# A gated graph network and a graph attention layer: two transposes moved from TensorE to DMA, a broadcast moved from DMA to TensorE

## The chip, the cores and the metric

The kernel runs on one core of one Trainium2 chip. A core has five engines that are of interest here: TensorE (PE in the profile: matrix products, and transposes as products with an identity), VectorE (DVE), ScalarE (ACT), GpSimd (POOL) and SyncE (SP), which issues nearly all of the DMAs. Each engine runs its own instructions strictly in their order and waits on semaphores for those of others. The metric is the device time in microseconds, lower is better.

## The reference

There are 64 graphs of 256 nodes with 256 features, in float32. Layer 0 is a gated graph network of three steps, layer 1 one step of graph attention; each starts from a layer norm and a relu, and is added to its input.

```python
h = relu(layernorm(x)); h0 = h                  # "first h" of a graph
for i in range(3):
    m = h @ weight[i]
    aggr = A.T @ m                              # A = (adj != 0)
    h = gru_cell(aggr, h, w_ih, w_hh, b_ih, b_hh)
x = x + h
h = relu(layernorm(x)) @ W.T
e = leaky_relu((h @ a_left)[:, :, None] + (h @ a_right)[:, None, :])
e = where(adj == 0, -1e9, e)
x = x + softmax(e, axis=-1) @ h
```

## The kernel before, in words

Graphs go through two at a time (G = 2), in 32 pairs. A tile of class "full" or "round" is 128 partitions by 512 elements: either the two halves of one graph's nodes with nodes on partitions, or both graphs of the pair with half of the features on partitions ("transposed").

Layer 0 works on the transposed form. First h comes out of the norm with nodes on partitions (`norm_relu`, L498) and is transposed ("turn 0", "turn 1", L525: four 128x128 transposes on TensorE for each half of the features, then a copy out of the bank by ScalarE, "turn copy", L529). In each of three steps `split` (L316, L443 to L445) cuts h into parts in a rounded format, "prop" (L543) multiplies by the adjacency, and `gate` (L458, the scale on ScalarE L472, L463) forms the gates; "back" (L586) transposes h back to nodes on partitions.

Layer 1: after the second norm VectorE forms the left and right scores of each node ("dot", L608) as columns of a small tile. The right scores have to stand along the free axis of all partitions. Before, for all pairs but the last, they are written as a line to DRAM ("line", L617) and read back as a broadcast over 128 partitions ("right", L620); in the last pair TensorE transposes the column spread over 128 columns (L628). "leaky" on ScalarE (L632) adds left and right and applies the leaky relu, "mask" (L635) and "max" (L637) run on VectorE, "exps" (L644) on ScalarE for both graphs. The attention weights are transposed ("p turn", L659: four TensorE transposes a graph; "p copy", L663: ScalarE), multiplied by h ("mix", L668), projected by W ("project", L677), added ("out", L682) and stored (L685).

The order of the instructions is not written by hand. Every operation is entered in a `Plan` with its engine, the time it occupies the engine, a latency, its reads and writes and the fixed leads of a table. `Plan.run` then places the operations one by one, always the one that can start earliest, over a window of four pairs, so that layer 1 of one pair is interleaved with layer 0 of the next ones; tiles are handed out in the same pass, from 28 tiles "full", 32 "round" and 8 PSUM banks. The start of an operation follows from these lines:

```python
for q in o.preds:
    t = max(t, q.start + q.occ if q.eng == e else q.end)
```

The costs in the plan decide the order alone; on the chip each engine runs in this order and waits for what is late.

Of the kernel before, what the change touches and what calls it, by code (L numbers as in the profile page):

```python
# [10 lines left out]
F32 = mybir.dt.float32  # L11
F32R = mybir.dt.float32r
I32 = mybir.dt.int32
AF = mybir.ActivationFunctionType
ALU = mybir.AluOpType
AX = mybir.AxisListType
# [176 lines left out]
def tile_gated_gnn_then_gat(  # L193
# [35 lines left out]
    nc = tc.nc  # L229
    P = 128  # L230
# [4 lines left out]
    G = 2  # L235
# [12 lines left out]
    plan.slot_class("x", [const.tile([P, GN], F32, name=f"x{i}") for i in range(2)])  # L248
    plan.slot_class("adj", [const.tile([P, GN], I32, name=f"adj{i}") for i in range(2)])
    plan.slot_class("small", [const.tile([P, 32], F32, name=f"small{i}") for i in range(12)])  # L250
    dram = ctx.enter_context(tc.tile_pool(name="dram", bufs=1, space=bass.MemoryType.DRAM))
    plan.slot_class("line", [dram.tile([1, N], F32, name=f"line{i}") for i in range(4)])
    plan.slot_class("bank", [psum.tile([P, GN], F32, name=f"bank{i}") for i in range(8)])

    ALL = (0, 1)
# [193 lines left out]
    def gate(name, e, terms, tops, apart=False, bias=0.0):  # L449
# [24 lines left out]
        pe(name + " rest", 2 * PASS * len(terms), rest, r=reads((2,), 1), w=[(bank, ONE)])  # L474
        return bank

    def norm_relu(name, src, dst):

        sm = Buf("small")
        st = lambda k: sm.t[:, 6 * k : 6 * k + 6]  # L480
        mv = lambda: sm.t[:, 12:16].rearrange("p (k s) -> p k s", s=2)

        def stats():
            for nb in range(NB):
                nc.vector.bn_stats(st(nb), parts(src)[:, nb, :])
            for nb in range(NB):
                nc.vector.bn_aggr(mv()[:, nb, :], st(nb))

        dve(name + " stats", 900, stats, r=[(src, ALL)], w=[(sm, (0, 1))])
        dve(name + " eps", 70, lambda: nc.vector.tensor_scalar(sm.t[:, 16:18], mv()[:, :, 1], LN_EPS, None, op0=ALU.add),  # L490
            r=[(sm, (0, 1))], w=[(sm, (2,))])
        pool(name + " pow", 900, lambda: nc.gpsimd.tensor_tensor(sm.t[:, 16:18], sm.t[:, 16:18], nhalf, ALU.pow),  # L492
             r=[("nhalf", ONE)], w=[(sm, (2,))])
        dve2(name + " shift", 70, lambda: nc.vector.scalar_tensor_tensor(sm.t[:, 18:20], mv()[:, :, 0], -1.0, sm.t[:, 16:18],
                                                       op0=ALU.mult, op1=ALU.mult),
            r=[(sm, (0, 1, 2))], w=[(sm, (3,))])
        for nb in range(NB):
            act(name + " relu", 495, lambda nb=nb: nc.scalar.activation(  # L498
                parts(dst)[:, nb, :], parts(src)[:, nb, :], AF.Relu,
                bias=sm.t[:, 18 + nb : 19 + nb], scale=sm.t[:, 16 + nb : 17 + nb]),  # L500
                r=[(src, (nb,)), (sm, (2, 3))], w=[(dst, (nb,))])

    def pair(p):
# [12 lines left out]
            dve2(f"in lo {g}", V512, lambda g=g, hi=hi, lo=lo: nc.vector.tensor_sub(lo[g].t, h[g].t, hi[g].t.bitcast(F32)),  # L516
                r=[(h[g], ALL), (hi[g], ONE)], w=[(lo[g], ONE)])
        hT = [Buf("full") for _ in range(DB)]
        for db in range(DB):
            pt = Buf("bank")  # L520

            def turn(db=db, pt=pt):
                for g in range(G):
                    for nb in range(NB):
                        nc.tensor.transpose(pt.t[:, (g * NB + nb) * P : (g * NB + nb + 1) * P],  # L525
                                            parts(h[g])[:, nb, ts(db, P)], ident)

            pe(f"turn {db}", TR * 4, turn, r=[(b, ALL) for b in h] + [("ident", ONE)], w=[(pt, ONE)])
            act(f"turn copy {db}", A512, lambda db=db, pt=pt: nc.scalar.copy(hT[db].t, pt.t), r=[(pt, ONE)], w=[(hT[db], ALL)])  # L529
# [71 lines left out]
        for g in range(G):  # L601
            pool("fill", 520, lambda b=pm_[g]: nc.gpsimd.memset(b.t, NEG_INF), w=[(pm_[g], ALL)])
            norm_relu(f"mid {g}", XR[g], hb[g])
            sm = sms[g]
            for nb in range(NB):
                for n in range(2):
                    c = 12 + n * NB + nb
                    dve2(f"dot {g}", 425, lambda g=g, nb=nb, n=n, c=c, sm=sm: nc.vector.scalar_tensor_tensor(  # L608
                        parts(sc[g])[:, nb, :], parts(hb[g])[:, nb, :], 1.0, va[:, n, :], op0=ALU.mult, op1=ALU.mult,
                        accum_out=sm.t[:, c : c + 1]),  # L610
                        r=[(hb[g], (nb,)), ("va", ONE)], w=[(sm, (c,)), (sc[g], (nb,))])

            if p < NPAIR - 1:
                line, pR = Buf("line"), Buf("full")
                plan.op(f"line {g}", "SP", 150, 2800, lambda line=line, sm=sm: nc.sync.dma_start(  # L617
                    line.t.rearrange("o (nb q) -> (o q) nb", q=P), sm.t[:, 12 + NB : 12 + 2 * NB]),
                    r=[(sm, (14, 15))], w=[(line, ONE)])
                plan.op(f"right {g}", "SP", 150, 2600, lambda line=line, pR=pR: nc.sync.dma_start(  # L620
                    pR.t[:, :N], line.t.to_broadcast([P, N])), r=[(line, ONE)], w=[(pR, ONE)])
            else:
                pR = Buf("bank")

                def right(sm=sm, pR=pR):
                    for nb in range(NB):
                        c = 12 + NB + nb
                        nc.tensor.transpose(pR.t[:, ts(nb, P)], sm.t[:, c : c + 1].to_broadcast([P, P]), ident)  # L628

                pe(f"right {g}", 2 * TR, right, r=[(sm, (14, 15))], w=[(pR, ONE)])  # L630
            for nb in range(NB):
                act(f"leaky {g}", 365, lambda b=sc[g], nb=nb, pR=pR, sm=sm: nc.scalar.activation(  # L632
                    parts(b)[:, nb, :], pR.t[:, :N], AF.Prelu, bias=sm.t[:, 12 + nb : 13 + nb], alpha=LEAKY_SLOPE),
                    r=[(pR, ONE), (sm, (12 + nb,))], w=[(sc[g], (nb,))])
            dve2(f"mask {g}", 660, lambda g=g: nc.vector.copy_predicated(pm_[g].t, A[g].t.bitcast(I32), sc[g].t),  # L635
                r=[(A[g], ONE), (sc[g], ALL)], w=[(pm_[g], ALL)])
            dve(f"max {g}", 610, lambda b=pm_[g], sm=sm: nc.vector.tensor_reduce(sm.t[:, 0:NB], parts(b), AX.X, ALU.max, negate=True),  # L637
                r=[(pm_[g], ALL)], w=[(sm, ONE)])
# [11 lines left out]
        for g in range(G):  # L650
            sm = sms[g]
            dve("recip", 70, lambda sm=sm: nc.vector.reciprocal(sm.t[:, 8 : 8 + NB], sm.t[:, 4 : 4 + NB]),
                r=[(sm, (1,))], w=[(sm, (2,))])
            pt, pT, pg, ag, pv = Buf("bank"), Buf("full"), Buf("bank"), Buf("full"), Buf("bank")

            def turn(g=g, pt=pt):
                for jb in range(NB):
                    for ib in range(NB):
                        nc.tensor.transpose(pt.t[:, (jb * NB + ib) * P : (jb * NB + ib + 1) * P],  # L659
                                            parts(pm_[g])[:, ib, ts(jb, P)], ident)  # L660

            pe(f"p turn {g}", 4 * TR, turn, r=[(pm_[g], ALL)], w=[(pt, ONE)])
            act(f"p copy {g}", A512, lambda pt=pt, pT=pT: nc.scalar.copy(pT.t, pt.t), r=[(pt, ONE)], w=[(pT, ONE)])  # L663

            def mix(g=g, pT=pT, pg=pg):
                for db in range(DB):
                    for jb in range(NB):
                        nc.tensor.matmul(pg.t[:, ts(db, N)], parts(hb[g])[:, jb, ts(db, P)], pT.t[:, ts(jb, N)],  # L668
                                         start=(jb == 0), stop=(jb == NB - 1))

            pe(f"mix {g}", 4 * MM, mix, r=[(pT, ONE), (hb[g], ALL)], w=[(pg, ONE)])
            act(f"mix copy {g}", A512, lambda ag=ag, pg=pg: nc.scalar.copy(ag.t, pg.t), r=[(pg, ONE)], w=[(ag, ONE)])

            def project(ag=ag, pv=pv):
                for ib in range(NB):
                    for db in range(DB):
                        nc.tensor.matmul(pv.t[:, ts(ib, D)], ag.t[:, db * N + ib * P : db * N + (ib + 1) * P],  # L677
                                         wT[:, db, :], start=(db == 0), stop=(db == DB - 1))

            pe(f"project {g}", 4 * MM, project, r=[(ag, ONE)] + WT, w=[(pv, ONE)])  # L680
            for nb in range(NB):
                dve(f"out {g}", VP256, lambda b=XR[g], nb=nb, pv=pv, sm=sm: nc.vector.scalar_tensor_tensor(  # L682
                    parts(b)[:, nb, :], pv.t[:, ts(nb, D)], sm.t[:, 8 + nb : 9 + nb], parts(b)[:, nb, :],
                    op0=ALU.mult, op1=ALU.add), r=[(pv, ONE), (sm, (2,))], w=[(XR[g], (nb,))])
            dma("store", 256, lambda g=g, b=XR[g]: nc.sync.dma_start(rows(out, G * p + g), parts(b)), r=[(XR[g], ALL)])  # L685
# [36 lines left out]
```

## Time and profile before

| | |
|---|---|
| runs | 2807.66 us median of 3 (2804.49 to 2813.82) |
| profiled execution | 2807.66 us, its span 2805.9 us |
| TensorE busy | 2312.1 us, 82% |
| VectorE busy | 1832.8 us, 65% |
| ScalarE busy | 1677.4 us, 60% |
| TensorE clock granted, mean | 0.898 |
| right broadcast, x62 | 128 KB, 4.8 us from issue to landing |
| line, x62 | 1 KB, 9.1 us from issue to landing |
| turn, TensorE, x256 | 39.9 us busy; its copy on ScalarE x64, 585 ns each |
| p turn, TensorE, x256 | 35.8 us busy; its copy on ScalarE x64, 591 ns each |

In a line of waits the engine and its tile and line stand first, then what it waited for, then the sum of the waits in us, how many they are, and the longest. In a line of a timeline the first two numbers are the start and the duration in us, and what stands in brackets is the idle time before it. A matmul's duration contains the pipeline, so the distance between starts is the better measure of its cost.

### The profile page before, as it was taken

How to read it: one execution, taken by the hardware profiler on the slowest of the kernel's cores; microseconds unless marked ns; L12 is line 12 of the kernel's file. 1: busy time of each engine (PE TensorE's matmuls, PEld its weight loads, DVE VectorE, ACT ScalarE, POOL GpSimd, SP SyncE). 2: the span in 40 equal slices, each digit the busy share in tenths (PEclk: the TensorE clock that was granted, in tenths of full speed). 3: DMA queues.
4: the chain of work that ended last, by engine and by line, in shares of the span. 5: the costliest groups of instructions: out<-in, count | busy, mean ns of one | idle time of the engine just before them, and what ended most of it. 6: DMA issues, size and time to landing. Idle time of an engine off the chain costs nothing. (4 is left out here: it accounts for less than half of the span.)

```text
span 2805.9 us, 30945 instructions
## 1 busy us (share of the span) xinstructions
PE 2312.1 (82%) x10853; PEld 1886.9 (67%) x10853; DVE 1832.8 (65%) x4084; ACT 1677.4 (60%) x3069; POOL 136.8 (5%) x198
## 2 busy tenths in 40 slices
PE   8987778877789777897777987778977789877786
PEld 6766667766677666676666776667766667666665
DVE  8766666765667556676566766566765667666654
ACT  8665556655656556566565665565655656655654
POOL 1000000000000000000000000000000000000000
PEclk9988889988899888999888988889988999889897
DMA  2011111111111111111111111111111111111001
GB/s 83 23 34 19 23 31 32 32 27 21 25 33 32 31 23 19 34 31 34 19 20 34 32 33 24 22 28 33 32 31 23 19 35 31 34 19 23 16 18 25
DMA packets 98332, 79.93 MB, mean 28 GB/s; under 512 B 22128, under 2 KB 98176, under 8 KB 98176
## 3 DMA queue, kind: packets, MB, share of 16 engines
q1 hardware_dynamic: 98144, 77.95, 12.3%
q8 instruction: 85, 1.39, 0.2%
q14 instruction: 71, 0.58, 0.1%
q10 hardware_dynamic: 32, 0.01, 0.0%
HBM read 61.09 MB, written 16.84 MB: 28 GB/s over the span
## 5 line engine op out<-in xcount | busy, mean ns | idle before, releaser
L458 PE MATMUL bank<-round,fac_hh 128*128 128x512 f32 x2304 | 698.7, 434 | 298.5 <-ACT round L443 297.9
L458 PEld LDWEIGHTS bank<-round,fac_hh 128*128 128x128 f32 x2304 | 461.8, 209 | 405.4 <-ACT round L443 311.2
L458 PE MATMUL bank<-round,fac 128*128 128x512 f32 x2304 | 617.6, 402 | 0.0
L463 PE MATMUL bank<-round,fac_hh 128*128 128x512 f32 x1152 | 397.4, 427 | 156.6 <-ACT bank L472 156.6
L458 PEld LDWEIGHTS bank<-round,fac 128*128 128x128 f32 x2304 | 443.0, 193 | 104.6
L472 ACT ACTIVATE bank<-bank 128x512 f32<-128x512 f32 x576 | 332.7, 583 | 126.5 <-PE bank L458 123.8
L635 DVE COPY_PREDICATED full<-round,full 128x512 f32<-128x512 int32 x64 | 46.7, 730 | 512.5 <-ACT full L632 512.4
L632 ACT ACTIVATE full<-full,small 128x256 f32<-128x256 f32 x124 | 59.4, 503 | 527.5 <-DMA full<-line 527.5
L463 PE MATMUL bank<-round,fac 128*128 128x512 f32 x1152 | 372.6, 410 | 2.5 <-ACT bank L472 2.5
L463 PEld LDWEIGHTS bank<-round,fac_hh 128*128 128x128 f32 x1152 | 206.0, 195 | 213.7 <-ACT bank L472 184.8
L443 ACT CAST round<-full 128x512 fp32r<-128x512 f32 x384 | 234.5, 620 | 109.9 <-DVE full L316 109.9
L444 DVE TENSOR_TENSOR round<-full,full 128x512 fp32r<-128x512 f32 x384 | 261.9, 689 | 9.6
L463 PEld LDWEIGHTS bank<-round,fac 128*128 128x128 f32 x1152 | 221.3, 195 | 60.2 <-ACT bank L472 11.5
L445 DVE SCALAR_TENSOR_TENSOR round<-round,full 128x512 fp32r<-128x512 f32 x384 | 255.0, 685 | 3.4
L575 DVE TENSOR_TENSOR full<-full,full 128x512 f32<-128x512 f32 x192 | 132.3, 689 | 136.4 <-ACT full L569 136.3
L543 PE MATMUL bank<-round,round 128*128 128x256 f32 x1536 | 216.2, 283 | 0.7 <-DVE round L594 0.7
L543 PEld LDWEIGHTS bank<-round,round 128*128 128x128 f32 x1536 | 206.1, 189 | 15.0 <-DVE round L594 0.9
L566 ACT ACTIVATE full<-full,vec 128x512 f32<-128x512 f32 x192 | 138.9, 723 | 98.0 <-DVE full L565 94.2
L565 DVE TENSOR_TENSOR full<-full,bank 128x512 f32<-128x512 f32 x192 | 131.6, 686 | 74.4 <-PE bank L463 67.2
L492 POOL TENSOR_TENSOR small<-small,nhalf 128x2 f32<-128x2 f32 x128 | 97.0, 758 | 1626.5 <-DVE small L490 1530.4
L316 DVE TENSOR_SCALAR full<-full 128x512 int32<-128x512 int32 (+1 forms) x400 | 163.0, 421 | 10.8 <-ACT full L547 5.0
L594 DVE TENSOR_TENSOR round<-bank,round 128x512 fp32r<-128x512 f32 x128 | 87.9, 688 | 117.7 <-ACT round L593 115.5
(75 smaller groups left out, 2883.2 us busy)
## 6 DMA issues: line engine op xcount, KB each, us to landing
x<-in_x_dram SPq DMA_DIRECT2D x64, 256.0 KB, 2.8
adj<-in_adj_dram SPq DMA_DIRECT2D x64, 256.0 KB, 2.7
full<-in_x_dram SPq DMA_DIRECT2D x64, 256.0 KB, 3.1
out_dram<-full SPq DMA_DIRECT2D x64, 256.0 KB, 2.1
full<-line SPq DMA_DIRECT2D x62, 128.0 KB, 4.8
line<-small SPq DMA_DIRECT2D x62, 1.0 KB, 9.1
full<-in_L_gnn_w_ih_dram SPq DMA_DIRECT2D x3, 256.0 KB, 4.0
full<-in_L_gnn_weight_dram SPq DMA_DIRECT2D x3, 256.0 KB, 4.7
```

What stands on the lines that cost most here:

```text
L316: dve2(name, 60 + n * 0.54, lambda: nc.vector.tensor_scalar(dst().bitcast(I32), src().bitcast(I32), CUT, None, op0=ALU.bitwise_and), r=r, w=w)
L443: act(name + " 0", C512, lambda: nc.scalar.copy(v0.t, t.t), r=[(t, ONE)], w=[(v0, ONE)])
L444: dve2(name + " 1", V512, lambda: nc.vector.tensor_sub(v1.t, v.t, t.t), r=[(v, ALL), (t, ONE)], w=[(v1, ONE)])
L445: dve2(name + " d", V512, lambda: nc.vector.scalar_tensor_tensor(vd.t, v1.t.bitcast(F32), -SPLIT, t.t, op0=ALU.mult, op1=ALU.add), r=[(v1, ...
L458: nc.tensor.matmul(bank.t, f(m, j, kb), b.t, start=(first and n == 0), stop=True, skip_group_check=True)
L463: nc.tensor.matmul(bank.t, f(m, 2, kb), s[kb][2].t, start=False, stop=True, skip_group_check=True)
L472: act(name + " scale", A512, lambda: nc.scalar.activation(bank.t, bank.t, AF.Identity, bias=bias, scale=1.0 + C), r=[("vec", ONE)], w=[(ba ...
L492: pool(name + " pow", 900, lambda: nc.gpsimd.tensor_tensor(sm.t[:, 16:18], sm.t[:, 16:18], nhalf, ALU.pow), r=[("nhalf", ONE)], w=[(sm, (2 ...
L543: nc.tensor.matmul(pa.t[:, ts(g, N)], parts(b)[:, sb, ts(db, P)], parts(A[g])[:, sb, :], start=(n == 0), stop=(n == len(terms) - 1))
L565: dve(f"u add {db}", V512, lambda u=u, k=pn: nc.vector.tensor_add(u.t, u.t, k.t), r=[(pn, ONE)], w=[(u, ONE)])
L566: act(f"tanh {db}", 615, lambda u=u, en=en: nc.scalar.activation(u.t, u.t, AF.Tanh, bias=b_i[:, en : en + 1]), r=[("vec", ONE)], w=[(u, ONE)])
L575: dve2(f"d mul {db}", V512, lambda d=d, b=z_: nc.vector.tensor_mul(d.t, d.t, b.t), r=[(z_, ONE)], w=[(d, ALL)])
```

## The change

Two things are done together. Right scores are spread by TensorE in all pairs, as they were in the last one, and the DRAM line and its tiles are gone. First h (for all pairs but the first) and the attention weights (for all pairs but the last) are no longer transposed by TensorE. Instead the 32-bit tile is seen as 16-bit halves: one DMA transpose turns 128 x 1024 halves into eight blocks of 128 x 128, in which low and high halves stand on alternating partitions; eight plain DMAs gather the even and odd partitions of each block to where they belong, low and high halves in separate columns; and a copy on ScalarE, over 1024 16-bit elements, interleaves them again ("join"). All of these DMAs are issued by SyncE.

```diff
-    plan.slot_class("line", [dram.tile([1, N], F32, name=f"line{i}") for i in range(4)])
+    def dma_turn(name, src, dst, region):
+        t = Buf("full")
+        view = lambda: t.t.bitcast(U16).rearrange("p (k c n) -> p k c n", k=NB, n=P)
+        plan.op(name, "SP", 200, 4500, lambda: nc.sync.dma_start_transpose(
+            t.t.bitcast(U16).rearrange("p (c n) -> p c n", n=P), src.t.bitcast(U16)), r=[(src, ALL)], w=[(t, ONE)])
+        def gather(c):
+            for q in range(2):
+                for half in range(2):
+                    nc.sync.dma_start(dst(c, slice(64 * q, 64 * q + 64))[:, half].rearrange("p (k n) -> p k n", k=NB),
+                                      view()[half::2, :, 2 * c + q, :])
+        for c in range(2):
+            plan.op(name + " gather", "SP", 500, 3500, lambda c=c: gather(c), r=[(t, ONE)], w=[region(c)])
+    def join(name, src, dst):
+        act(name, 980, lambda: nc.scalar.copy(
+            dst.t.bitcast(U16).rearrange("p (j n b) -> p j n b", j=2, b=2),
+            src.t.bitcast(U16).rearrange("p (j b n) -> p j n b", j=2, b=2)), r=[(src, ALL)], w=[(dst, ALL)])
...
-        for db in range(DB):
+        if p > 0:
+            rs = [Buf("full") for _ in range(DB)]
+            for g in range(G):
+                dma_turn(f"turn {g}", h[g], lambda db, rows, g=g, rs=rs: rs[db].t[rows].bitcast(U16).rearrange(
+                    "p (g b n) -> p g b n", g=G, b=2)[:, g], lambda db, g=g, rs=rs: (rs[db], (g,)))
+            for db in range(DB):
+                join(f"turn copy {db}", rs[db], hT[db])
+        for db in range(DB if p == 0 else 0):
...
-            if p < NPAIR - 1:
-                line, pR = Buf("line"), Buf("full")
-                plan.op(f"line {g}", "SP", 150, 2800, lambda line=line, sm=sm: nc.sync.dma_start(
-                    line.t.rearrange("o (nb q) -> (o q) nb", q=P), sm.t[:, 12 + NB : 12 + 2 * NB]),
-                    r=[(sm, (14, 15))], w=[(line, ONE)])
-                plan.op(f"right {g}", "SP", 150, 2600, lambda line=line, pR=pR: nc.sync.dma_start(
-                    pR.t[:, :N], line.t.to_broadcast([P, N])), r=[(line, ONE)], w=[(pR, ONE)])
-            else:
-                pR = Buf("bank")
-                def right(sm=sm, pR=pR):
-                    for nb in range(NB):
-                        c = 12 + NB + nb
-                        nc.tensor.transpose(pR.t[:, ts(nb, P)], sm.t[:, c : c + 1].to_broadcast([P, P]), ident)
-                pe(f"right {g}", 2 * TR, right, r=[(sm, (14, 15))], w=[(pR, ONE)])
+            pR = Buf("bank")
+            def right(sm=sm, pR=pR):
+                for nb in range(NB):
+                    c = 12 + NB + nb
+                    nc.tensor.transpose(pR.t[:, ts(nb, P)], sm.t[:, c : c + 1].to_broadcast([P, P]), ident)
+            pe(f"right {g}", 2 * TR, right, r=[(sm, (14, 15))], w=[(pR, ONE)])
...
-            pe(f"p turn {g}", 4 * TR, turn, r=[(pm_[g], ALL)], w=[(pt, ONE)])
-            act(f"p copy {g}", A512, lambda pt=pt, pT=pT: nc.scalar.copy(pT.t, pt.t), r=[(pt, ONE)], w=[(pT, ONE)])
+            if p < NPAIR - 1:
+                rs = Buf("full")
+                dma_turn(f"p turn {g}", pm_[g], lambda jb, rows, rs=rs: rs.t[rows].bitcast(U16).rearrange(
+                    "p (j b n) -> p j b n", j=NB, b=2)[:, jb], lambda jb, rs=rs: (rs, (jb,)))
+                join(f"p copy {g}", rs, pT)
+            else:
+                pe(f"p turn {g}", 4 * TR, turn, r=[(pm_[g], ALL)], w=[(pt, ONE)])
+                act(f"p copy {g}", A512, lambda pt=pt, pT=pT: nc.scalar.copy(pT.t, pt.t), r=[(pt, ONE)], w=[(pT, ALL)])
```

In the order that the planner makes of the changed kernel, SyncE's queue for one pair reads: two transposes of attention weights, their 16 gathers, two stores, two loads of x, a load of adj, the transpose of first h of one graph, its 8 gathers, a load of x and of adj, the transpose of first h of the other graph, its 8 gathers, a load of x.

More of the change, by code (lines that the diff above doesn't have):

```diff
@@ L13 @@
 I32 = mybir.dt.int32
+U16 = mybir.dt.uint16
 AF = mybir.ActivationFunctionType
@@ L250, in tile_gated_gnn_then_gat @@
     plan.slot_class("small", [const.tile([P, 32], F32, name=f"small{i}") for i in range(12)])
-    dram = ctx.enter_context(tc.tile_pool(name="dram", bufs=1, space=bass.MemoryType.DRAM))
-    plan.slot_class("line", [dram.tile([1, N], F32, name=f"line{i}") for i in range(4)])
     plan.slot_class("bank", [psum.tile([P, GN], F32, name=f"bank{i}") for i in range(8)])
@@ L653, in pair @@
                 r=[(sm, (1,))], w=[(sm, (2,))])
-            pt, pT, pg, ag, pv = Buf("bank"), Buf("full"), Buf("bank"), Buf("full"), Buf("bank")
+            pT, pg, ag, pv = Buf("full"), Buf("bank"), Buf("full"), Buf("bank")
+            pt = Buf("bank")
             def turn(g=g, pt=pt):
@@ L669, in mix @@
                                          start=(jb == 0), stop=(jb == NB - 1))
-            pe(f"mix {g}", 4 * MM, mix, r=[(pT, ONE), (hb[g], ALL)], w=[(pg, ONE)])
+            pe(f"mix {g}", 4 * MM, mix, r=[(pT, ALL), (hb[g], ALL)], w=[(pg, ONE)])
             act(f"mix copy {g}", A512, lambda ag=ag, pg=pg: nc.scalar.copy(ag.t, pg.t), r=[(pg, ONE)], w=[(ag, ONE)])
```

## The prediction

> **What bounds the kernel now.** I read the waits first, because TensorE is busy for 82% of the span and the question is what the rest is.
>
> ```profile
> ACT full L632 <- DMA full<-line: 527.5, 62, 15.6
> DVE full L635 <- ACT full L632: 512.4, 61, 15.3
> PE bank L458 <- ACT round L443: 297.9, 30, 15.2
> PE bank L463 <- ACT bank L472: 159.1, 38, 13.0
> ```
>
> 62 times (twice in each of 31 pairs) ScalarE stands for 8.5 us until the broadcast of the right-hand scores lands. TensorE's two large idle groups (297.9 and 159.1 us, together 14.7 a pair) name ScalarE's cast and scale, which are queued behind that wait. Then stretches of 10 us, columns PE, PEld, DVE, ACT, POOL busy, granted clock, DMA share, GB/s:
>
> ```profile
> 1000.00:1010.00 10.00, 2.66 (x15) 1.94 (x13) 0.50 (x1) 1.38 (x3) 0.00 (x0) 0.74 0.07 14
> 1010.00:1020.00 10.00, 3.78 (x8) 2.48 (x8) 2.78 (x5) 2.42 (x6) 0.00 (x0) 0.50 0.28 13
> 1020.00:1030.00 10.00, 8.27 (x33) 6.77 (x34) 9.04 (x17) 9.94 (x21) 1.26 (x2) 0.74 0.00 0
> 1030.00:1040.00 10.00, 10.00 (x49) 8.50 (x48) 6.07 (x11) 5.97 (x12) 0.00 (x0) 1.00 0.03 9
> 1040.00:1050.00 10.00, 10.00 (x51) 8.36 (x50) 4.43 (x9) 4.91 (x9) 0.00 (x0) 1.00 0.32 97
> ```
>
> Outside the two waits TensorE is never idle and has its full clock; inside them it is idle, and the clock falls to 0.50 and stays there for some 4 us after work resumes. Summed by microsecond over 87 us, a pair's period (86.25 us: the 31 first broadcasts are issued from 139.24 to 2726.84) is 67.2 us of TensorE work at full clock, 15.3 idle and 3.75 lost to the half clock. The timelines of ScalarE around the place where the change puts new waits:
>
> ```profile
> 1062.42 1.08 ACT L498 ACTIVATE full<-x,small 128x256 f32<-128x256 f32 x2
> ...
> 1067.01 0.59 ACT L498 ACTIVATE full<-x,small 128x256 f32<-128x256 f32 x1
> ...
> 1070.12 0.63 ACT L443 CAST round<-full 128x512 fp32r<-128x512 f32 x1
> 1070.64 0.67 ACT L472 ACTIVATE bank<-bank,vec 128x512 f32<-128x512 f32 x1
> ```
>
> First h of the two graphs is ready at 1063.5 and 1067.6, seven microseconds before the instruction at 1070.64.
>
> **What the Trainium skill says.** "TensorE: Matmul & The Clock Gate", What's actually happening: after an idle window of about 3.4 us the clock halves. The trace agrees: 0.50 from 2 to 4 us into each gap. "DMA: Bandwidth & Descriptors", Issuing engines are not separate DMA queues, and Two DMAs through the same engine are not ordered: a dependent DMA has to wait, on the issuing engine, for the first one's completion. The trace shows this: SyncE waits 554.9 us in 62 times for the first DMA of the pair (line) before it issues the second.
>
> **Why the planner did not see the stall, before or after.** `Plan.run` lets an operation start after a predecessor on its own engine at `q.start + q.occ`, after others at `q.end`. Line and right are both SP operations, so right is planned 150 ns after line, and line's 2800 are never counted. The changed kernel has the same pattern: a transpose and its gathers are all SP, so the gathers are planned 200 ns after the transpose; its 4500 counts nowhere. ScalarE's joins stand too early by a whole DMA transpose.
>
> **The change, part by part, for one pair.** T is the time from issue to landing of one DMA transpose of 256 KB, which no trace here shows.
>
> 1. Removed: the line and right DMAs, with 15.3 us idle and 3.75 of half clock.
> 2. TensorE: 16 transposes fewer (turn and p turn; four start within 0.36 us, 1068.34 to 1068.70, so 1.44 us), 4 more for right (0.36). Work 67.2 - 1.1 = 66.1 us. The new right can wait for VectorE's dots in TensorE's queue; VectorE is 65% busy, I cost that at nothing, up to 1 us a pair without that cover.
> 3. ScalarE: four joins of 1024 elements for four copies of 585 and 591 ns. From 384 elements at 530 ns (L377) and 512 at 620 (L443), 0.70 ns an element, a join takes 980 ns; the page "ScalarE: Activation LUTs", What ACT_TABLE_LOAD costs, gives 186 + 0.833 x 1024 = 1039. I take 1.0. The 1.6 us more hide in ScalarE's 40% idle time except where it is late, which is counted below.
> 4. SyncE: 4 transposes and 32 gathers for 4 DMAs. A load occupies the queue for 0.37 us (row of L305); 8 gathers take 3.0. A load of 256 KB lands in 2.8 us, with 16 packets on each DMA engine at 54 ns (share 0.32 of 160 engine-us for 97 GB/s of 1 KB packets), so 1.9 is fixed. A gather has 8 packets an engine: 1.9 + 0.4 = 2.3 us.
> 5. Attention weights. From the end of exps (time 0) ScalarE has five scales, a cast, a table load (1.28) and a sigmoid ahead of the first join, at the starts seen (0.5 each, 0.6 the sigmoid) 4.9 us. Graph 0's weights are ready at -1.1; transposed at T - 1.1; 8 gathers issued by T + 1.9, landed T + 4.2. Wait: T - 0.7. Graph 1's gathers go behind them on the queue: landed T + 7.1, 1.9 after the first join's end. TensorE stands at mix 0 for the whole first wait; mix 0 itself (1.7 us) covers part of the second: 1.2 idle. Sum T + 0.5.
> 6. First h. The first transpose is issued at 1063.5; its gathers block SyncE until T has passed, then take 3.0, then two loads 0.74; only now, at 1067.2 + T, does the second transpose go. It lands at 1067.2 + 2T; four gathers 1.5 and 2.3: 1071.0 + 2T. The join's place on ScalarE, behind the same L443, is 1070.6. Wait: 2T + 0.4. TensorE has 4.0 us of released work by then, and ScalarE needs 3.0 after the wait (join, copy, join, scale) to release more: 2T - 0.6 idle.
>
> Idle in all 3T - 0.1 us a pair. For T the lower bound is a load of the same bytes, 2.8; the page "Advanced Engine Details and Errata", X-Bar Transpose (TRN2), calls transposes as fast as regular DMAs. The upper one is eight blocks in a row at the 1309 ns of "VectorE: DVE Perf Modes", The three transpose paths: 10.5. I take 4.3, an estimate: 1.9 fixed, 1.0 for the bytes at the 261 GB/s of "DMA: Bandwidth & Descriptors", Latency and other measured facts, and 1.4 for descriptors of 256 bytes. Idle is then 12.8, the half clock costs 3.4 (the first gap is shorter than before's), the period is 66.1 + 12.8 + 3.4 = 82.3 us: 3.95 less than 86.25, x31 = 122. The span of 2805.9 becomes 2684. The profiled run took 2807.66, which is also the median of the three runs, 1.8 more than its span: 2686 us.
>
> **Rivals.** *Slow transposes*: new idle passes the old at T = 5.5 (16.4 + 3.8 against 15.3 + 3.75 + 1.1), and each further us costs 3 x 31 = 93 us. For it: nothing hides T, and it is serial twice at first h. Against it: the pages' bandwidths. T = 7.5 gives 22.4 + 4: 3004 us; 10.5 gives 3290. *Transposes like loads*: T = 2.8, idle 8.3, half clock 2.5: 2519 us. *Hidden anyway*: the gathers' latency is planned and h is wanted by the splits only some 3 us later, so if ScalarE reached the joins late enough, little would be left; S = 2 gives 2246. Against it, the tight places of steps 5 and 6. *Slow gathers*: packets of 256 bytes landing like line's (9.1 us, median) would add 6.8 twice, 13.6 us a pair, 3108 us; but line writes 4-byte pieces to HBM, the gathers 256 bytes to SBUF.
>
> **How the numbers follow.** Within 0.3%, about 8 us, is about what a measurement of this kernel can tell from no change. My case (T from 3.3 to 5.3; its own range 2565 to 2790) has 0.42, T lower or partly hidden 0.15, slow transposes 0.29, slow gathers or a new queue wait 0.10, and 0.04 falls within 0.3% around T = 5.5. Faster 0.57, same 0.04, slower 0.39. The range from 2450 to 3060 leaves out the fully hidden case and T over 8.
>
> **What would show it.** Right: no wait for a broadcast; two waits of ScalarE a pair ending on gathers, one of about T + 2 after exps, one of about 2T at first h, with the second transpose issued only after the first's gathers; TensorE's clock at 0.50 in two places a pair; transposes landing in 4 to 5 us. Wrong: T outside 3 to 5.5; gathers landing over 3 us; SyncE busy for more than 0.4 us a gather; joins much over 1 us; or ScalarE reaching the joins so late that it waits for nothing.

## The result

| | before | changed |
|---|---|---|
| median | 2806.07 us (2803.83 to 2813.82) | 2850.98 us (2843.94 to 2853.46) |
| ratio | | 1.0151, 95% interval 1.0123 to 1.0179 |
| span of the profiled execution | 2805.9 us | 2847.4 us |
| TensorE busy | 2312.1 us | 2325.8 us |
| mean clock granted | 0.898 | 0.902 |

The kernel became 1.5% slower; the interval is clear of 1. 2686 us and "faster" were forecast. The time lies inside the range of 2450 to 3060 us, but above the time of the kernel before, not below it. In the waits of the changed kernel the broadcast is gone, and the joins stand where it stood:

```profile
ACT full L496 <- DMA full<-full: 569.6, 123, 11.9
PE bank L462 <- ACT bank L471: 301.1, 32, 11.3
PE bank L697 <- ACT full L496: 177.1, 62, 5.4
```

ScalarE waits 18.4 us a pair at the joins (569.6 over 31; before 17.0 at the broadcast). TensorE's idle time is again in two groups: 301.1 us behind the joins of first h (its gates wait for the scale, L471, which stands behind the joins), and 177.1 us at mix (L697), which reads the joined weights. Together 15.4 us a pair, against 14.7 in the two groups of before. The stretches of 10 us, in the columns of before:

```profile
1000.00:1010.00 10.00, 6.56 (x40) 5.46 (x38) 5.95 (x13) 1.59 (x3) 0.69 (x1) 1.00 0.42 102
1010.00:1020.00 10.00, 3.66 (x9) 2.88 (x10) 4.19 (x12) 5.07 (x8) 0.79 (x1) 0.58 0.20 51
1020.00:1030.00 10.00, 10.00 (x46) 8.22 (x45) 8.40 (x24) 8.96 (x18) 0.00 (x0) 0.91 0.00 1
1030.00:1040.00 10.00, 10.00 (x48) 8.12 (x47) 9.93 (x23) 8.65 (x19) 0.00 (x0) 1.00 0.17 33
1040.00:1050.00 10.00, 6.25 (x26) 4.75 (x25) 3.81 (x6) 5.29 (x7) 0.00 (x0) 0.95 0.30 63
1050.00:1060.00 10.00, 7.91 (x20) 5.77 (x19) 2.67 (x4) 5.12 (x8) 0.99 (x2) 0.53 0.05 11
```

Two gaps a pair, each followed by a stretch at half clock. Summed by microsecond over three whole periods, a pair is 66.7 us of TensorE's work at full clock, 16.0 idle and 5.0 lost to the half clock; the same sum over three periods of the kernel before gives 67.5, 15.3 and 4.05. The gain in TensorE's work (0.8 us) is there; idle time and half clock took back more than that.

What fills the gaps is seen on SyncE's queue (start, duration of the whole row; L482 is the transpose, L488 the gather, L304 a load) and beside it on ScalarE (L521 makes first h, L665 is exps, L496 the join):

```profile
994.54 1.27 SPq L482 DMA_TRANSPOSE full<-full  x1
997.67 5.17 SPq L488 DMA_DIRECT2D full<-full  x8
1002.88 0.60 SPq L304 DMA_DIRECT2D x<-in_x_dram  x1
1003.58 0.41 SPq L304 DMA_DIRECT2D adj<-in_adj_dram  x1
1004.08 1.27 SPq L482 DMA_TRANSPOSE full<-full  x1
1008.10 5.17 SPq L488 DMA_DIRECT2D full<-full  x8
...
1037.11 2.64 SPq L482 DMA_TRANSPOSE full<-full  x2
1040.40 10.35 SPq L488 DMA_DIRECT2D full<-full  x16
```

```profile
993.44 1.08 ACT L521 ACTIVATE full<-x,small 128x256 f32<-128x256 f32 x2
...
1012.09 1.16 ACT L496 COPY full<-full 128x1024 uint16<-128x1024 uint16 x1 [10.38 <-DMA full<-full]
...
1037.48 0.50 ACT L665 ACTIVATE full<-full,small 128x256 f32<-128x256 f32 x1
...
1047.15 1.16 ACT L496 COPY full<-full 128x1024 uint16<-128x1024 uint16 x1 [2.53 <-DMA full<-full]
1052.36 1.16 ACT L496 COPY full<-full 128x1024 uint16<-128x1024 uint16 x1 [4.05 <-DMA full<-full]
```

First h of the first graph is ready at 994.52. The second graph's transpose goes at 1004.08 only, after the first one's landing, its eight gathers and two loads; the join starts at 1012.09, after a wait of 10.38. The weights (transposes at 1037.11, then all 16 gathers) cost two waits, 2.53 and 4.05. Eight gathers occupy the queue for 5.17 us: this is the number that was not foreseen.

### The profile page after: what moved, and what is told of

Its sections match the earlier page's. It is cut to its first block, busy times and chain, and to the rows that moved or that the text cites. A ratio compares the mean times of both kernels' runs of the same rounds, so it can differ in the third digit from the quotient of the medians.

```text
span 2847.4 us, 32298 instructions
## 1 busy us (share of the span) xinstructions
PE 2325.8 (82%) x10481; PEld 1878.3 (66%) x10481; DVE 1829.1 (64%) x4084; ACT 1731.4 (61%) x3069; POOL 130.1 (5%) x198
## 4 chain that ended last, share of the span: by engine, by line
PE 40%; SPq 16%; DMA 13%; DVE 13%; ACT 12%; issue 5%; ACTq 0%; DVEq 0%; POOLq 0%; POOL 0%
PE bank L457 19%; SPq L488 16%; DMA full<-full 13%; PE bank L462 9%; PE bank L706 4%; PE bank L573 3%; PE bank L697 3%; DVE round L444 2%; ACT bank L471 2%; DVE round L443 2%; ACT full L521 2%; DVE small L508 1%; ACT full L496 1%; ACT L665 1%; ACT full L665 1%
## 5 line engine op out<-in xcount | busy, mean ns | idle before, releaser
L457 PE MATMUL bank<-round,fac_hh 128*128 128x512 f32 x2304 | 643.3, 408 | 2.0 <-DVE round L443 2.0
L462 PE MATMUL bank<-round,fac_hh 128*128 128x512 f32 x1152 | 388.4, 419 | 300.8 <-ACT bank L471 300.8
L457 PEld LDWEIGHTS bank<-round,fac 128*128 128x128 f32 x2304 | 472.6, 206 | 116.0 <-ACT round L442 0.7
L496 ACT COPY full<-full 128x1024 uint16<-128x1024 uint16 x124 | 144.0, 1161 | 569.6 <-DMA full<-full 569.6
L457 PEld LDWEIGHTS bank<-round,fac_hh 128*128 128x128 f32 x2304 | 427.4, 192 | 89.2 <-DVE round L443 2.5
L462 PEld LDWEIGHTS bank<-round,fac_hh 128*128 128x128 f32 x1152 | 210.3, 195 | 345.7 <-ACT bank L471 309.0
L471 ACT ACTIVATE bank<-bank 128x512 f32<-128x512 f32 x576 | 328.6, 583 | 162.1 <-PE bank L457 156.1
L462 PE MATMUL bank<-round,fac 128*128 128x512 f32 x1152 | 348.1, 396 | 0.3 <-ACT bank L471 0.3
L697 PE MATMUL bank<-full,full 128*128 128x256 f32 x512 | 198.6, 556 | 177.1 <-ACT full L496 177.1
L592 DVE TENSOR_TENSOR full<-bank,full 128x512 f32<-128x512 f32 x192 | 131.2, 683 | 314.2 <-ACT full L588 310.3
L697 PEld LDWEIGHTS bank<-full,full 128*128 128x128 f32 x512 | 135.1, 276 | 237.4 <-ACT full L496 211.4
L462 PEld LDWEIGHTS bank<-round,fac 128*128 128x128 f32 x1152 | 214.1, 188 | 55.7 <-ACT bank L471 7.4
L599 ACT ACTIVATE full<-bank,b_rz 128x512 f32<-128x512 f32 x192 | 132.2, 689 | 84.9 <-PE bank L462 84.9
```

The source lines that it names most:

```text
L457: nc.tensor.matmul(bank.t, f(m, j, kb), b.t, start=(first and n == 0), stop=True, skip_group_check=True)
L462: nc.tensor.matmul(bank.t, f(m, 2, kb), s[kb][2].t, start=False, stop=True, skip_group_check=True)
L471: act(name + " scale", A512, lambda: nc.scalar.activation(bank.t, bank.t, AF.Identity, bias=bias, scale=1.0 + C), r=[("vec", ONE)], w=[(ba ...
L496: act(name, 980, lambda: nc.scalar.copy(dst.t.bitcast(U16).rearrange("p (j n b) -> p j n b", j=2, b=2), src.t.bitcast(U16).rearrange("p (j ...
```

## The experiments

The theory: TensorE's idle time, before and after, is ScalarE standing at a DMA whose time the planner leaves out, and the size of the new stall is set by the landing of the transposes and by what SyncE pays for the gathers. Rivals: the idle time belongs to the dense schedule itself; the DMAs are too long to be hidden in any order; the two new places disturb one another on the queue. Ratios are to runs of the kernel before on the same chip, whose medians were 2783, 2807 and 2773 us in the three groups of runs. A run without an interval was timed once. Where an edit changes what is planned, the planner also makes a new order of it; only the runs with first h turned twice and with four gathers keep the order of the changed kernel.

### One part at a time

For the run without either stall, the conditions of the DMA transposes are replaced:

```diff
-        if p > 0:
+        if False:
-        for db in range(DB if p == 0 else 0):
+        for db in range(DB):
-            if p < NPAIR - 1:      # weights
+            if False:
```

The second run has only the last of these edits, the third only the first two.

> Right scores by TensorE as in the changed kernel, but both transposes left on TensorE: neither the DMA broadcast nor the DMA transposes are there. Theory (all idle time of TensorE in both kernels comes from ScalarE standing at a DMA): idle and half clock go, about 67.3 us a pair are left, span near 2218 us, clock above 0.98. Rival (part of the idle time belongs to the dense schedule itself, or a steadier load makes the clock fall): 2300 us or more.

> The changed kernel with the attention weights left on TensorE; only first h is transposed by DMA. Theory: one gap a pair at the joins of first h, 9.7 us idle and some 2.5 us of half clock, less 0.7 us of TensorE work: 2218 + 31 x 11.5 = 2575 us. Rival (the two places wait for each other on SyncE's queue, so that one alone is nearly free): under 2450 us.

> The changed kernel with first h left on TensorE; only the attention weights are transposed by DMA. Theory: 5.8 us idle and some 2 us of half clock a pair, less 0.7: 2218 + 31 x 7.1 = 2440 us. Rival (as above, nearly free alone): under 2330 us.

Measured: 2248.5 us (0.808 of the kernel before), clock 0.996, TensorE busy for 99% of the span; 2612.2 us (0.939); 2500.4 us (0.899). So the dense schedule runs at full clock and hardly idles, and the theory's sum was 30 us too low. First h costs 364 us or 11.7 a pair over the first run, the weights 252 us or 8.1, each somewhat more than expected. In ratios they add up to 0.131 + 0.091 = 0.221, and the changed kernel stands 0.207 over the first run: the two places are nearly independent, and neither is nearly free alone.

### The same DMAs in an order that counts them

```diff
-                        t = max(t, q.start + q.occ if q.eng == e else q.end)
+                        t = max(t, q.start + q.occ if q.eng == e and e != "SP" else q.end)
-        plan.op(name, "SP", 200, 4500, lambda: nc.sync.dma_start_transpose(
+        plan.op(name, "SP", 1300, 4000, lambda: nc.sync.dma_start_transpose(
-            plan.op(name + " gather", "SP", 500, 3500, ...)
+            plan.op(name + " gather", "SP", 2600, 4200, ...)
-        act(name, 980, ...)
+        act(name, 1070, ...)
```

> The changed kernel, the same DMAs and joins; only the planner is told what they take: an SP operation after another SP operation waits for its end, a transpose occupies SP 1.3 us and lands after 4.0, four gathers occupy 2.6 and land after 4.2, a join takes 1.07. Theory (the DMAs can be hidden, the joins only stand too early on ScalarE): no waits of more than 2 us at the joins, 66 to 68 us a pair, 2170 to 2240 us. Rival (the DMA chain is too long for the window of pairs and the 28 tiles, or SyncE's queue becomes the bound): 2500 us or more.

Measured: 2320.5 us, ratio 0.8334 (0.8318 to 0.8351). The landings are the same (gathers 1.9 us, transposes 3.3, medians), and no join waits for a DMA any more (569.6 us before this edit); the largest group of waits of TensorE is this:

```profile
PE bank L462 <- ACT bank L471: 88.2, 61, 1.7
```

Changing what the planner counts, which changes only the order, is worth 18% here. The time is still 80 us over what was expected at most: TensorE stops for 1.4 us twice in each pair, for ScalarE's scale (L471), which here waits for no DMA. That the order itself holds this gap is likely, but no run here shows the plan's own times. The same repair was given to the kernel before, where line and right follow each other on SyncE:

```diff
-                plan.op(f"line {g}", "SP", 150, 2800, ...)
-                plan.op(f"right {g}", "SP", 150, 2600, ...)
+                plan.op(f"line {g}", "SP", 400, 9100, ...)
+                plan.op(f"right {g}", "SP", 400, 4800, ...)
```

> The kernel before, with line and right still by DMA; only the planner is told that an SP operation after another one waits for its end, and that line lands after 9.1 us and right after 4.8. Theory (the same error of the plan made the stall of the kernel before): no waits for the broadcast, about 2250 us. Rival (the round trip is too long to be hidden in any order): 2600 us or more.

Measured: 2266.0 us, ratio 0.8071 (0.8057 to 0.8085), and ScalarE's waits for the broadcast fell from 527.5 us in 62 times to three:

```profile
ACT full L632 <- DMA full<-line: 2.4, 3, 1.7
```

Both stalls had one cause. Most of what the two kernels lost to the version without these DMAs was lost to the order, not to the DMAs' length.

### How the transposes of first h count

```diff
+        def turn_it():
+            for _ in range(times):          # 2 for first h, 1 for the weights
+                nc.sync.dma_start_transpose(...)
-        plan.op(name, "SP", 200, 4500, lambda: nc.sync.dma_start_transpose(...), ...)
+        plan.op(name, "SP", 200, 4500, turn_it, ...)
```

> The changed kernel in the same order, but each DMA transpose of first h is done twice, the second after the first has landed (some 4 us later). Theory (the transposes of the two graphs stand one behind the other in SyncE's queue, each landing counts in full): 8 us a pair more, 2850 + 248 = 3098 us. Rival (the two overlap, one landing counts): 4 us a pair, 2974 us. Rival (hidden): 2850 us.

Measured: 3052.4 us, 201 more. SyncE (second graph of a pair) and ScalarE in this run:

```profile
1095.39 5.01 SPq L484 DMA_TRANSPOSE full<-full  x2
1102.24 5.17 SPq L491 DMA_DIRECT2D full<-full  x8
```

```profile
1106.31 1.16 ACT L499 COPY full<-full 128x1024 uint16<-128x1024 uint16 x1 [17.26 <-DMA full<-full]
```

Summed over both graphs and taken as a mean over the 31 pairs, 13.6 us pass from the transposes to their first gathers instead of 7.15, and the first wait at the joins is 17.0 us instead of 10.6. Both grew by 6.4, that is 2 x 3.2, and x31 it gives about 200. Both landings count in full, one behind the other, as the theory has it; only a transpose costs about 3.2 us there, not the 4 put in. One landing alone would have given half of that.

### What a gather costs SyncE

The weights of a graph go into another order of columns, (half, row block, column block, n), which lets one DMA take four runs a partition instead of two:

```diff
+                for half in range(2):
+                    nc.sync.dma_start(
+                        whole()[64 * c : 64 * c + 64].bitcast(U16)[:, 512 * half : 512 * half + 512].rearrange("p (m n) -> p m n", n=P),
+                        t.t.bitcast(U16).rearrange("p (m n) -> p m n", n=P)[half::2, c::2, :])
```

> The changed kernel in the same order on every engine, but the attention weights of a graph are gathered by four DMAs of 64 KB instead of eight of 32 KB (the column blocks lie in another order, which mix reads accordingly). Theory (SyncE pays about 0.65 us for each gather, whatever it carries): graph 0's gathers take 2.6 us less and graph 1's 5.2 less, the two waits at the joins of the weights all but vanish (idle of TensorE there from 5.8 us a pair to under 1), with the half clock some 7 us x 31: 2630 us. Rival (the cost goes with packets or bytes): a gather takes some 1.2 us, time 2820 to 2860 us.

Measured: 2661.8 us (0.948), 189 less than the changed kernel and 32 more than the theory said. A gather of 64 KB occupies the queue as long as one of 32 KB, by these two rows (min, median, max in ns), the larger one first:

```profile
L488 SPq DMA_DIRECT2D full<-full x248: 593/614/698, 170.2 to 2605.1; - x124
L494 SPq DMA_DIRECT2D full<-full x496: 593/605/1110, 41.0 to 2507.7; - x166
```

The wait at the first join of the weights is gone in most pairs, that at the second fell to some 1.5 us, and TensorE's at mix went from 177.1 us to

```profile
PE bank L703 <- ACT full L502: 63.3, 59, 3.2
```

These are 2.0 us a pair where under 1 was expected, because the second wait stays; x31 that is about the 32 us. So the number of gathers counts, not their bytes. What in a gather makes it dearer than the 0.37 us that the prediction took from the loads was asked by DMAs of several shapes after the end of the work:

> Right scores and transposes by TensorE, and after the end of the work DMAs of several shapes in rows, four or eight of each, whose results nobody uses; only their times on SyncE's queue and their landing count, the run's time says nothing. Shapes: the gather as it is (64 partitions by steps of 2, two runs of 128 16-bit elements); the same from 64 neighbouring partitions; the same bytes as 32-bit elements; one run of 512 bytes; 128 neighbouring partitions; 256 KB from SBUF in runs of 1 KB; 256 KB from HBM; transposes of 256 KB and of 32 KB. If the step of 2 makes a gather's 0.605 us, the second shape takes 0.37; if the element size, the third; if the number of runs, the fourth; if it is the source in SBUF, all SBUF copies take 0.6 and the load 0.37.

```profile
L732 SPq DMA_DIRECT2D full<-fac_hh x8: 600/606/719, 2245.6 to 2250.2; - x8
L734 SPq DMA_DIRECT2D full<-fac_hh x8: 604/606/615, 2250.9 to 2255.5; - x8
L736 SPq DMA_DIRECT2D full<-fac_hh x8: 593/606/607, 2256.2 to 2260.8; - x8
L738 SPq DMA_DIRECT2D full<-fac_hh x8: 594/595/602, 2261.4 to 2265.9; - x8
L740 SPq DMA_DIRECT2D full<-fac_hh x4: 620/620/622, 2266.6 to 2268.6; - x4
L742 SPq DMA_DIRECT2D full<-fac_hh x4: 619/626/641, 2269.2 to 2271.2; - x4
L744 SPq DMA_DIRECT2D full<-in_x_dram x4: 402/490/616, 2271.9 to 2273.7; - x4
```

In the order of the expectation: the gather, neighbouring partitions, 32-bit elements, one run, 128 partitions, 256 KB from SBUF, 256 KB from HBM. Every copy from SBUF to SBUF takes 0.60 to 0.63 us, whatever its stride, element, runs and size; the load from HBM takes 0.49 in the middle, falling from 0.62 to 0.40 along its row of four. Neither stride nor size is to blame. Nor is the source in SBUF alone, as the expectation put it: the kernel before stores 256 KB from SBUF to HBM, and such a store takes

```profile
L685 SPq DMA_DIRECT2D out_dram<-full x64: 377/378/383, 174.7 to 2802.7; - x64
```

Nor is it the place in a row: of the changed kernel's 992 gathers none takes less than 0.593, the first behind each transpose's landing included. So it is the copy within SBUF that costs SyncE this much. Why it does, and why a load right behind gathers also takes 0.60 (1002.88 above), the runs don't tell.

### The best that came out of it

The first run has both repairs, the plan that counts and four gathers for the weights; the second the same, with first h on TensorE; the third is the first experiment's kernel, timed.

> Both repairs at once: the plan counts the landings of SP operations, and the weights of a graph are gathered by four DMAs. Theory (what is left of the 2320 us of the repaired plan over the 2248 of all TensorE is idle time of TensorE that the longer queue of gathers forces into the order): between the two, about 2290 us. Rival (the 72 us are a price of the DMA traffic itself): 2320 us.

> As the run before, but first h is transposed by TensorE; the weights alone go by DMA, in four gathers, with the plan that counts them. Theory: the queue is short, nothing waits, TensorE has 0.7 us a pair less than with all transposes on it: 2225 to 2250 us. Rival: DMA transposes cost even when hidden, 2280 us.

> Both transposes and the right scores on TensorE, timed: 2248 us as in its one run, the fastest of all or level with the run before this one.

Measured: 2256.35 us, ratio 0.8136 (0.8122 to 0.8149); 2236.29 us, 0.8065 (0.8053 to 0.8077); 2248.01 us, 0.8108 (0.8096 to 0.8120). Eight gathers fewer a pair, with the same bytes, take away most of the 72 us that the repaired plan still lost, so these were no price of the bytes moved; TensorE's group at L462 fell with them from 88.2 to 22.3 us. With only the weights by DMA the kernel is 0.5% faster than with everything on TensorE. First h by DMA is not worth its queue. One thing stays open: 0.8065 is level with the 0.8071 of the kernel before whose plan alone was repaired. In microseconds the two are 2236 and 2266, but they were timed on different chips. So whether moving the weights gains anything over the repaired kernel before is not shown.

## Why the prediction was wrong

**What bounds the kernel** held. TensorE idles where ScalarE stands at a DMA: without the two new and the two old places it is busy for 99% of the span. So did the reading of the planner's line: with it and the landing times put right, both kernels lose these waits.

**The failed step is step 4, the price of a gather on SyncE.** "A load occupies the queue for 0.37 us (row of L305); 8 gathers take 3.0": they take 5.17, 0.65 from start to start. The mechanism was right and this term was mis-sized, because a load from HBM was taken for copies within SBUF, of which the trace of before had none, and no upper bound was drawn for it. Over 0.4 us a gather is one of the signs of being wrong that the prediction itself names. For the weights the cause is shown by an experiment: with eight gathers instead of sixteen for the weights of a pair, which take 8 x 0.65 = 5.2 us where 5.9 was forecast, the same kernel comes to 0.948 of the one before, on the side that was forecast. For first h the number of gathers was not varied; there it rests on the sum in the next paragraph.

**Step 6, first h**, from the relu's end to the join: 16.1 us were forecast (2T + 7.5), 17.6 measured. The two transposes took 7.15 to their first gathers instead of 8.6, the twelve gathers 7.8 instead of 4.5, the two loads 1.24 instead of 0.74, and the last landing the remaining 1.4 instead of 2.3. The gathers alone are 3.3 us over; the transposes and the last landing, put too high, took 2.3 of that back. The second graph's h was ready some 3 us before its place on ScalarE, not seven as the reading of the timeline says of both; as its transpose stands behind the first graph's gathers, this changed nothing. ScalarE came 7.2 us after the relu, as said (7.1). The wait became 10.4 instead of 9.0, TensorE's idle time 9.7 instead of 8.0.

**Step 5, the weights**: the second join was forecast at T + 7.1 = 11.4 us after exps, and came at 14.4: 16 gathers took 10.35 us instead of 5.9, and shorter landings took 1.4 of these 4.4 back. ScalarE reached the first join after 6.65 us, not 4.9, because its scales waited for TensorE (1.26 us at one of them) and were not back to back. This took something off the first wait (2.5, not 3.6), and the second became 4.05 instead of 1.9. Idle 5.7, not 4.8.

**T** was an estimate of 4.3: the transposes land 3.3 us after issue in the median (3.1 to 4.9), and in the pair shown 3.1 to 4.0 pass to the first gather. The estimate lay between its bounds, and T nearer the load's 2.8; of the 4.3, the 1.4 for descriptors of 256 bytes had no working behind it. This error made the forecast slower, not faster: by the prediction's own formula, 3T - 0.1, the T measured and 0.37 us a gather would have given less idle time still. "Slow transposes", the rival on which slower rested, is not what happened. "Slow gathers" is what happened, in another form: they land in 1.9 us, quicker than the 2.3 put in, and are slow to issue. "Hidden anyway" (S there is the idle time left in a pair, as its sum shows) is not what happened either: ScalarE waited at 123 of the 124 joins.

**Half clock**: 5.0 us a pair, 3.4 forecast. The second gap of the weights falls into the half clock after the first one (0.53 in the stretch from 1050 to 1060).

**Steps 2 and 3**: TensorE's work fell by 0.8 us (1.1 forecast); a join takes 1161 ns, not the 1000 taken. The new right transposes held TensorE up in the last pair alone, as in the kernel before (6.0 us in all).

Altogether idle 16.0 for 12.8, half clock 5.0 for 3.4, work 66.7 for 66.1: 5.4 us a pair more than 82.3, which turns a forecast gain of 4 us a pair into a loss of 1.3 (mean period 87.57, before 86.25).

## What to carry to other kernels

In a list scheduler, a DMA and the operation that needs its data may be issued by the same engine, and yet the second starts at the end of the first, not after its issue: this one line, together with the landing times measured, was worth 18 and 19% in two kernels. Before DMAs are put in place of compute, count them and multiply by what the issuing queue pays for that very kind of transfer; merging 32 gathers a pair into 24 took 6.6% off the changed kernel, with the same bytes moved. When a stall is removed by moving work, ask whether the replacement waits in the same in-order queue at the same kind of place.

## What was not expected of the hardware

A DMA from SBUF to SBUF occupies SyncE's queue for about 0.6 us whether it carries 32 or 256 KB, in one run or two, while a store from SBUF to HBM takes 0.38 and a load from HBM behind no other DMA 0.37. A DMA transpose of 256 KB of 16-bit data occupies the queue for 1.27 us and lands in 3.3 us (median of 124), one of 32 KB lands in 2.4 (issued in a row of four, 1.3 us apart): eight times the data costs about 0.9 us more, so eight blocks one after another (the upper bound of 10.5) was far off. A copy of 1024 16-bit elements on ScalarE takes 1161 ns.
